# A fused attention and mixture-of-experts block: expert tile pairs cut in two halves and spread over 98 steps, scatters at three a step

## The chip, the core and the metric

The kernel runs on one core of a Trainium2 chip. Its time is the device time of one execution in microseconds (us); the kernel before takes 1445.82 us, the median of three runs (1444.02 to 1447.47).

## What is computed

One transformer block on x of shape (4, 1024, 256), all in float32: a layer norm without weights, then attention and a mixture of experts, both on the normed rows, and the sum of all three.

```python
xn = layernorm(x)
# attention: 16 heads of 16, rotary embedding, softmax over all 1024 keys
qkv = xn @ W_qkv + b_qkv
out = softmax(q @ k.T / sqrt(16)) @ v            # per batch and head
attn = out @ W_out + b_out
# mixture of experts: 16 experts, 4 per token, 256 -> 128 -> 256
scores = sigmoid(xn @ w_gate.T)                   # top 2 of 4 groups, then top 4 experts
g, u = silu(xn @ w1_e.T), xn @ w3_e.T
routed = sum over the 4 experts of weight * ((g * u) @ w2_e.T)
shared = (silu(xn @ w1s.T) * (xn @ w3s.T)) @ w2s.T
return x + attn + routed + shared
```

## The kernel before

**Steps.** Attention is the frame. There are 4 batches of 4 groups of 4 heads, and a group takes 16 steps, so 256 steps in all. `Attention.step` (line 1329) writes one of them. It issues four score products `ps` with the exponential on ScalarE behind each (`exp_one`, line 1170) and four products `pm` of the next group with their row maxima on VectorE behind them (`max_one`, line 1125): half of these eight at the start, half at the end. In the middle, in `between`, it runs the step's *units*: pieces of other work that are handed in as closures. Behind the second half comes `av_part`, the product of the exponentials of the step before with the values. It is written whole if the next step has a unit; otherwise it is cut in two, and the second part goes into the middle of that next step.

**What sets the order.** Every TensorE instruction is kept in the order in which it is written (`Kit.pe`, line 289); TensorE never runs a later unit before an earlier one. The same holds for most of SyncE's transfers (`Kit.sp`, line 295), while the expert loads are placed behind the last transfer written (`issue_after(k.last_sp)`, line 876). All PSUM tiles come from one pool of eight banks.

**Units.** The function `pieces` (line 219) lists the units of a step. First stand attention's own (the projection of the next batch at every second step, its transposes three steps later, the maxima's transposes, the normalisation of a finished group, the output projection); then the shared expert; then the routed experts. The shared expert has 16 blocks of 256 rows with three units each (`shared_block`, line 789): two `hidden` and a `last`. The first 36 units come from step 10 on at three in seven steps (until step 92), the other 12 once the routed experts are done, at two in five steps.

**The routed experts** take four stages.

1. The routing, computed from step 9 on, gives each token's four slots in a buffer `xs` in HBM in which the rows lie sorted by expert.
2. From step 33 on, `put` (line 848) scatters rows into `xs`: 128 indirect DMAs of 128 rows, issued by GpSimd, two a step, so the last one is in step 96. Each is tied to one of the step's maxima or exponentials as its pace (`Kit.paced`).
3. From step 98 on, 72 *pairs* of expert tiles (256 rows each) are worked off, one a step, by `expert_units` (line 871). The unit `pair_of(i)` (line 922) holds, in this order: `outer(i - 1)`, the second product `exy` of the pair before, whose stationary operand is that pair's `gu`; `load(i + 2)`, the rows and the two experts' weights; `turn(i + 1)`, the transposes `ext` of the next pair's rows; `hidden` of pair i (line 759). The last unit is `outer(71)`, at step 170.
4. From step 171 on, `get` (line 940) gathers the results from `ys`, 128 indirect DMAs, two a step (one a step from step 240 on), and `add` sums them on VectorE.

**Inside `hidden`.** Sixteen matmuls `ph_r` are followed by three instructions in a row: tanh on ScalarE (line 776), and two on VectorE (lines 777 and 779). The second of these writes `gu_r`.

```python
th = self.ff.tile([P, SL], F32, name=f"th_{tag}", tag="th")
nc.scalar.activation(th, ph[:, 0, :], AF.Tanh, scale=0.5)
nc.vector.scalar_tensor_tensor(th, th, 1.0, ph[:, 0, :], ALU.add, ALU.mult)
gu = self.ff.tile([P, SL], F32, name=f"gu_{tag}", tag="gu", bufs=3)
nc.vector.tensor_tensor(gu, th, ph[:, 1, :], ALU.mult)
```

Of the kernel before, what the change touches and what calls it, by code (L numbers as in the profile page):

```python
# [20 lines left out]
NT = B * TT  # L21
# [4 lines left out]
TOPK_G, TOPK = 2, 4  # L26
# [6 lines left out]
PAIRS = (NT * P * TOPK // P + E - 1 + R - 1) // R  # L33
# [5 lines left out]
PROJECT = 29  # L39
ROUTE_FROM = 9  # L40
PUT_FROM = 33
TILES_FROM = 98
SHARED = ((10, 36),)
GET_AHEAD = 3
FILL_FROM, FILLS = 9, 8
FFN_AHEAD = 3
# [3 lines left out]
def kernel(  # L50
# [160 lines left out]
    beside = Beside(k, xnT, ff)  # L211
    routing_tensor = []
    routing = route(k, rt_pool, logits, routing_tensor)
    shared = beside.shared_units()
    n_put = NT * TOPK
    done = {"shared": 0}
    tiles, ex = None, None

    def pieces(step):

        nonlocal tiles
        now = norm.pieces(step, att.own(step))
        while routing_tensor:
            now.append(routing_tensor.pop(0))
        due = 0
        if SHARED[0][0] <= step:
            due = min(SHARED[0][1], 1 + (step - SHARED[0][0]) * 3 // 7)
        if tiles is not None and not tiles:
            due = min(len(shared), SHARED[0][1] + (step - TILES_FROM - PAIRS) * 2 // 5)
        while done["shared"] < due:  # L230
            now.append(shared[done["shared"]])
            done["shared"] += 1
        if step == TILES_FROM:
            tiles = beside.expert_units(ex.enter_context(ex_pool()))
        if tiles:
            now.append(tiles.pop(0))
            if not tiles:
                done["tiles"] = step
        return now

    def ex_pool():
        return tc.tile_pool(name="ex", bufs=2, side="right")
# [6 lines left out]

    ex = ExitStack()  # L250
    now = pieces(0)
    for step in range(STEPS):
        beside.tick()
        norm.moves(step)
        if step in k.at_step:
            with tc.issue_after(k.last_exp):
                k.at_step[step]()

        bits = []
        if routing is not None and step >= ROUTE_FROM:  # L260
            bits += [advance] * (1 if step >= PUT_FROM else 2 if k.ranking else 3)
        if step >= PUT_FROM and beside.put_next < n_put:
            assert k.slots_known
            bits[:0] = [beside.put] * 2
        if step > done.get("tiles", STEPS):
            if beside.got == 0:
                ex.close()
                beside.rows = att.rows = ctx.enter_context(
                    tc.tile_pool(name="gp", bufs=4, side="right")
                )  # L270
            for _ in range(2 if step < STEPS - 2 * TT else 1):
                bits += [beside.get, beside.add]
        then = pieces(step + 1) if step + 1 < STEPS else []
        att.step(now, bool(then), bits)
        now = then
# [461 lines left out]
class Beside:  # L737
# [109 lines left out]

    def put(self):
        k, nc, tc = self.k, self.nc, self.tc
        i = self.put_next  # L850
        self.put_next += 1
        t, kk = divmod(i, TOPK)
        q = t // QT
        if i == 0:
            self.fetch(0)
            self.fetch(1)
        elif i % (QT * TOPK) == 0 and q + 1 < NT // QT:
            self.fetch(q + 1)
        put = nc.gpsimd.indirect_dma_start(  # L859
            out=k.xs,  # L860
            out_offset=bass.IndirectOffsetOnAxis(ap=k.slot_i[:, t, kk : kk + 1], axis=0),
            in_=self.rows4[q][:, t % QT, :],
            in_offset=None,
        )
        k.paced(put.ins)

        tc.add_to_no_dep_group("put", put.ins)
        tc.declare_no_dep(put.ins, group="put", reason="rows of their own")


    def expert_units(self, ex):
        k, nc, tc = self.k, self.nc, self.tc
        got, xTs, gus = {}, {}, {}

        def load(i):
            with tc.issue_after(k.last_sp):
                xg = ex.tile([P, R, C], F32, name=f"xg_{i}", tag="xg")
                nc.sync.dma_start(
                    out=xg, in_=k.xs[i * SL : (i + 1) * SL, :].rearrange("(r p) c -> p r c", r=R)
                )  # L880
                w = ex.tile([P, R, WE], F32, name=f"w_{i}", tag="w", bufs=3)
                for r in range(R):
                    n = i * R + r
                    e = nc.sync.value_load(k.tile_e[0:1, n : n + 1], min_val=0, max_val=E - 1)
                    last = nc.sync.dma_start(out=w[:, r, :], in_=k.we[bass.ds(e * P, P), :])
            k.last_sp = last.ins
            got[i] = (xg, w)

        def turn(i):
            xg = got[i][0]  # L890
            pt = k.bank([P, NC_, R, P], f"ext_{i}")
            for c in range(NC_):
                for r in range(R):
                    k.pe(nc.tensor.transpose(pt[:, c, r, :], xg[:, r, c * P : (c + 1) * P], k.ident))  # L894
            xT = self.ff.tile([P, QT, C], F32, name=f"xT_{i}", tag="st")
            xTs[i] = xT[:, :NC_, :]
            nc.scalar.copy(xTs[i], pt.rearrange("p c r n -> p c (r n)"))  # L897

        def outer(i):
            py = k.bank([P, R, C], f"exy_{i}")  # L900
            for r in range(R):
                k.pe(
                    nc.tensor.matmul(  # L903
                        py[:, r, :], lhsT=gus[i][:, r * P : (r + 1) * P],
                        rhs=got[i][1][:, r, 2 * NC_ * F :], start=True, stop=True,
                    )
                )
            y = self.ff.tile([P, R, C], F32, name=f"y_{i}", tag="y", bufs=3)
            nc.scalar.activation(y, py, AF.Copy, scale=0.5)  # L909
            self.later.append(  # L910
                lambda: k.sp(
                    k.ys[i * SL : (i + 1) * SL, :].rearrange("(r p) c -> p r c", r=R), y
                )
            )

        def gate_and_up(i):
            gu = 2 * NC_ * F
            return [
                got[i][1][:, r, :gu].rearrange("p (n c f) -> n p c f", n=2, c=NC_) for r in range(R)
            ]  # L920

        def pair_of(i):
            def run():
                if i == 0:
                    for n in range(FFN_AHEAD - 1):
                        load(n)
                    turn(0)
                if i:
                    outer(i - 1)
                if i + FFN_AHEAD - 1 < PAIRS:  # L930
                    load(i + FFN_AHEAD - 1)
                if i + 1 < PAIRS:
                    turn(i + 1)
                gus[i] = self.hidden(xTs[i], gate_and_up(i), f"r{i}")
            return run

        return [pair_of(i) for i in range(PAIRS)] + [lambda: outer(PAIRS - 1)]


    def get(self):  # L940
# [513 lines left out]
```

## Time and profile before

| | |
|---|---|
| median of three runs | 1445.82 us |
| the profiled execution, its own time | 1442.6 us |
| its span, first to last instruction | 1440.8 us |
| mean granted TensorE clock | 0.995 |
| PE busy | 1407.5 us, 98% of the span |
| PEld (weight loads) busy | 685.6 us, 48% |
| VectorE (DVE) busy | 924.8 us, 64% |
| ScalarE (ACT) busy | 792.8 us, 55% |
| GpSimd (POOL) busy | 423.2 us, 29% |
| HBM traffic | 141 GB/s over the span |

The profile is taken in one execution. "PE" is TensorE's matmuls, "PEld" its weight loads, which overlap them. The row of a group of instructions gives its line in the kernel, the engine, the operation, the tiles written and read, how many there are, the busy time, the mean length of one in ns, and the idle time of the engine just before them with what ended it. In a timeline each row has its start and length in us, the engine and line, and in brackets the engine's idle time before it with its releaser. A float32 matmul shows as two instructions, a transpose as one.

The time of a step is read from the trace as the distance between the first `ps` matmuls of two steps. By this, step 46 begins at 335.5 us, step 81 at 499.3, step 98 at 577.5, step 171 at 1101.8, and step 240 at 1386.6. A step without any unit takes 3.53 us if the next has none either and 3.95 us if the next has one; a step with an expert pair and no other unit takes 6.42 us.

### The profile page before, as it was taken

To read this page: it belongs to the slowest core of one execution; us is meant where nothing else is said; L and a number is where in the kernel's file an instruction comes from. 1 tells how busy PE (TensorE), PEld (TensorE's weight loads), DVE (VectorE), ACT (ScalarE), POOL (GpSimd) and SP (SyncE) were. 2 spreads that over 40 slices of the span, in tenths; PEclk is the share of its full clock that TensorE was granted. 3 is DMA by queue.
4 is the path that set the end of the run, shared out by engine and by line. 5 is a ranking of instruction groups with operands and counts; after the bars stand their busy time and mean duration, and the time that the engine had idled before them with its cause. 6 is when DMAs were issued, how large, how long until landed. Compare 5 with 4: busy or idle time off the path is not lost.

```text
span 1440.8 us, 26647 instructions
## 1 busy us (share of the span) xinstructions
PE 1407.5 (98%) x9870; PEld 685.6 (48%) x9870; DVE 924.8 (64%) x1682; ACT 792.8 (55%) x1638; POOL 423.2 (29%) x498
## 2 busy tenths in 40 slices
PE   7699999999999999999999999999999999999998
PEld 4343344444444343566656665655665434433333
DVE  5667967667766676444555545555445888899941
ACT  5565554555554555555555555555555555566675
POOL 5401511574534546321000000001223444455400
PEclk9899999999999999999999999999999999999999
DMA  5132763333232223445666666665451334333310
GB/s 183 37 111 102 257 250 114 103 125 101 98 133 94 88 87 134 133 150 182 203 214 197 217 194 205 196 207 183 147 174 54 107 118 129 108 110 108 103 44 30
DMA packets 136673, 199.15 MB, mean 138 GB/s; under 512 B 13920, under 2 KB 99040, under 8 KB 136288
## 3 DMA queue, kind: packets, MB, share of 16 engines
q1 hardware_dynamic: 103088, 137.78, 29.8%
q0 software_dynamic: 12288, 33.57, 7.5%
q10 hardware_dynamic: 21168, 26.10, 5.2%
q8 instruction: 78, 1.28, 0.4%
q14 instruction: 51, 0.42, 0.1%
HBM read 124.01 MB, written 79.69 MB: 141 GB/s over the span
## 4 chain that ended last, share of the span: by engine, by line
PE 94%; ACT 3%; DVE 1%; DMA 0%; issue 0%; SPq 0%; ACTq 0%; DVEq 0%
PE pm L1135 22%; PE ps L1177 19%; PE av L1202 18%; PE ph_r L769 9%; PE exy L903 5%; PE ph_s L769 4%; PE pqk L1044 4%; PE ext L894 2%; PE pso L818 2%; PE py L1272 2%; PE pv L1044 2%; PE ptr L1118 2%; PE po L1226 1%; PE pmt L1158 1%; DVE mx L1143 1%; ACT other L373 1%
## 5 line engine op out<-in xcount | busy, mean ns | idle before, releaser
L1186 ACT ACTIVATE es<-ps 128x512 f32<-128x512 f32 x1024 | 555.0, 596 | 413.3 <-PE ps L1177 225.5
L1143 DVE TENSOR_REDUCE mx<-pm 128x1 f32<-128x512 f32 x1024 | 660.5, 684 | 181.2 <-PE pm L1135 115.3
L1135 PE MATMUL pm<-kT,qT 32*128 32x512 f32 x1792 | 522.8, 646 | 8.3 <-ACT kT L1123 5.6
L1177 PE MATMUL ps<-q,kT 32*128 32x512 f32 x1792 | 505.1, 640 | 0.9 <-DVE q L1163 0.8
L1202 PE MATMUL av<-es,vv 128*32 128x512 f32 (+1 forms) x2560 | 287.0, 519 | 0.0
L1177 PEld LDWEIGHTS ps<-q,kT 32*128 32x128 f32 x1792 | 142.3, 183 | 169.2 <-ACT es L1186 86.8
L1135 PEld LDWEIGHTS pm<-kT,qT 32*128 32x128 f32 x1792 | 157.0, 185 | 75.8 <-issue 24.9
L1202 PEld LDWEIGHTS av<-es,vv 128*32 128x32 f32 x2560 | 51.2, 108 | 239.6 <-issue 215.5
L859 POOL DMA_INDIRECT xs<-rows,slot_i x128 | 123.7, 967 | 125.3 <-DVE mx L1143 108.1
L950 POOL DMA_INDIRECT yg<-ys,slot_i x128 | 121.7, 951 | 127.6 <-DVE mx L1143 123.2
L777 DVE SCALAR_TENSOR_TENSOR th_r<-th_r,ph_r 128x256 f32<-128x256 f32 x72 | 30.3, 421 | 195.4 <-ACT th_r L776 195.4
L1082 POOL TENSOR_TENSOR rot<-qk,sin_sb 128x256 f32<-128x256 f32 x56 | 39.5, 726 | 369.4 <-DVE qk L1065 369.2
L769 PE MATMUL ph_r<-xT,w 128*128 128x128 f32 x1152 | 140.5, 275 | 0.5 <-ACT xT L897 0.5
L769 PEld LDWEIGHTS ph_r<-xT,w 128*128 128x128 f32 x1152 | 134.4, 192 | 0.8 <-ACT xT L897 0.7
L1135 PE MATMUL pm<-qkT,qkT 32*128 32x512 f32 x256 | 78.6, 640 | 1.3 <-DVE mx L1143 1.3
L903 PE MATMUL exy<-w,gu_r 128*128 128x256 f32 x288 | 77.3, 391 | 0.0
L1177 PE MATMUL ps<-q,qkT 32*128 32x512 f32 x256 | 75.3, 640 | 0.3 <-DVE gu_s L779 0.3
L776 ACT ACTIVATE th_r<-ph_r 128x256 f32<-128x256 f32 x72 | 27.6, 383 | 81.3 <-PE ph_r L769 81.3
L903 PEld LDWEIGHTS exy<-w,gu_r 128*128 128x128 f32 x288 | 50.0, 190 | 28.7 <-issue 19.7
L967 DVE SCALAR_TENSOR_TENSOR sum<-yg,wk,sum 128x256 f32<-128x256 f32 x128 | 61.4, 479 | 0.0
L909 ACT ACTIVATE y<-exy 128x512 f32<-128x512 f32 x72 | 43.7, 607 | 17.7 <-PE exy L903 17.4
L1036 POOL MEMSET vv<- 128x128 f32 x4 | 1.3, 316 | 143.2 <-ACT es L1186 143.2
(175 smaller groups left out, 1259.3 us busy)
## 6 DMA issues: line engine op xcount, KB each, us to landing
w<-we SPq DMA_DIRECT2D x144, 384.0 KB
xs<-zero ACTq DMA_DIRECT2D x8, 2304.0 KB
xg<-xs SPq DMA_DIRECT2D x72, 256.0 KB
ys<-y SPq DMA_DIRECT2D x72, 256.0 KB
acc<-acc SPq DMA_DIRECT2D x14, 512.0 KB
xb<-in_x_dram SPq DMA_DIRECT2D x16, 256.0 KB
acc<-xb SPq DMA_DIRECT2D x16, 256.0 KB
we<-in_w_dram ACTq DMA_DIRECT2D x4, 1024.0 KB
```

The costliest lines, as they stand in the source:

```text
L769: nc.tensor.matmul(ph[:, n, at], lhsT=w[n][:, c, :], rhs=xT[:, c, at], start=(c == 0), stop=(c == NC_ - 1),)
L859: put = nc.gpsimd.indirect_dma_start(out=k.xs, out_offset=bass.IndirectOffsetOnAxis(ap=k.slot_i[:, t, kk : kk + 1], axis=0), in_=self.rows ...
L903: nc.tensor.matmul(py[:, r, :], lhsT=gus[i][:, r * P : (r + 1) * P], rhs=got[i][1][:, r, 2 * NC_ * F :], start=True, stop=True,)
L909: nc.scalar.activation(y, py, AF.Copy, scale=0.5)
L950: get = nc.gpsimd.indirect_dma_start(out=self.yg[:, kk, :], out_offset=None, in_=k.ys, in_offset=bass.IndirectOffsetOnAxis(ap=k.slot_i[:, ...
L967: nc.vector.scalar_tensor_tensor(sm[:, 0, :], yg[:, kk, :], k.wk[:, t, kk : kk + 1], sm[:, 0, :], ALU.mult, ALU.add)
L1044: nc.tensor.matmul(ps[half][:, :w], lhsT=self.xnT[b][:, c, n0 : n0 + P], rhs=self.wqkv_sb[:, c, half * HALF : half * HALF + w], start=(c = ...
L1135: nc.tensor.matmul(ps, lhsT=self.qT[b, g // 2][rows, g % 2, qt * P : (qt + 1) * P], rhs=self.kT[b, g // 2][rows, g % 2, hf * HALF : (hf + ...
L1143: k.pace = nc.vector.tensor_reduce(out=self.mx_of[b, g, qt // 4][hf][:, qt % 4, j, :], in_=ps, axis=AX.X, op=ALU.max,).ins
L1177: nc.tensor.matmul(ps, lhsT=self.kT[b, g // 2][rows, g % 2, kc * P : (kc + 1) * P], rhs=self.q2[b, g, qh][rows, :], start=True, stop=True,)
L1186: k.last_exp = nc.scalar.activation(e, ps, AF.Exp, scale=DH**-0.5).ins
L1202: nc.tensor.matmul(av[32 * j : 32 * j + 32, cols], lhsT=self.vv[b][:, kc, h * VS : h * VS + 32], rhs=es[j][:, cols], start=(kc == 0), stop ...
```

## The change

The 72 pairs are cut into two units each: `around(i)` has the second product of the pair before, the load and the transposes, and `inner(i)` has `hidden`. With the last `outer` these are 145 units. They start at step 81 in place of 98, and by step `s` as many as `1 + (s - 81) * 144 // 98` have been handed out, so one or two a step, the last of them at step 179. The scatters go at two a step up to step 45 and at three from step 46 on, so that the last three are in step 79. The remaining shared units and the gathers follow the end of the tiles: the gathers start at step 180, and 8 of the 128 come after step 239, at one a step, until step 247. Nothing else changes: the same instructions run, with the same operands.

```diff
-TILES_FROM = 98
-SHARED = ((10, 36),)
+PUT_MORE = 46
+TILES_FROM, TILE_STEPS = 81, 98
+SHARED_FROM, SHARED_FIRST = 10, 36
...
-            due = min(len(shared), SHARED[0][1] + (step - TILES_FROM - PAIRS) * 2 // 5)
+            due = min(len(shared), SHARED_FIRST + (step - TILES_FROM - TILE_STEPS) * 2 // 5)
...
         if step == TILES_FROM:
             tiles = beside.expert_units(ex.enter_context(ex_pool()))
         if tiles:
-            now.append(tiles.pop(0))
+            due = 1 + (step - TILES_FROM) * (2 * PAIRS) // TILE_STEPS
+            while tiles and done["halves"] < due:
+                now.append(tiles.pop(0))
+                done["halves"] += 1
             if not tiles:
                 done["tiles"] = step
...
-            bits[:0] = [beside.put] * 2
+            bits[:0] = [beside.put] * (2 if step < PUT_MORE else 3)
...
     def put(self):
         k, nc, tc = self.k, self.nc, self.tc
+        if self.put_next == NT * TOPK:
+            return
...
-        def pair_of(i):
+
+        def around(i):
             def run():
                 if i == 0:
                     for n in range(FFN_AHEAD - 1):
...
                     load(i + FFN_AHEAD - 1)
                 if i + 1 < PAIRS:
                     turn(i + 1)
+            return run
+
+        def inner(i):
+            def run():
                 gus[i] = self.hidden(xTs[i], gate_and_up(i), f"r{i}")
             return run
 
-        return [pair_of(i) for i in range(PAIRS)] + [lambda: outer(PAIRS - 1)]
+        units = []
+        for i in range(PAIRS):
+            units += [around(i), inner(i)]
+        return units + [lambda: outer(PAIRS - 1)]
```

More of the change, by code (lines that the diff above doesn't have):

```diff
@@ L215 @@
     n_put = NT * TOPK
-    done = {"shared": 0}
+    done = {"shared": 0, "halves": 0}
     tiles, ex = None, None
@@ L225, in pieces @@
         due = 0
-        if SHARED[0][0] <= step:
-            due = min(SHARED[0][1], 1 + (step - SHARED[0][0]) * 3 // 7)
+        if SHARED_FROM <= step:
+            due = min(SHARED_FIRST, 1 + (step - SHARED_FROM) * 3 // 7)
         if tiles is not None and not tiles:
-            due = min(len(shared), SHARED[0][1] + (step - TILES_FROM - PAIRS) * 2 // 5)
+            due = min(len(shared), SHARED_FIRST + (step - TILES_FROM - TILE_STEPS) * 2 // 5)
         while done["shared"] < due:
```

## The prediction

> **What bounds the kernel.** I first read the page's busy rows.
>
> ```profile
> PE 1407.5 (98%) x9870; PEld 685.6 (48%) x9870; DVE 924.8 (64%) x1682; ACT 792.8 (55%) x1638; POOL 423.2 (29%) x498
> ```
>
> TensorE is busy in 98% of the span; no other engine comes above 64%. But a busy PE is a modelled figure, so the second view is the timeline of one step that carries an expert pair, TensorE's rows alone, from the end of the step's first half to its end. Columns: start and length in us, engine, line, operation.
>
> ```profile
> 728.40 1.13 PE L903 MATMUL exy<-w,gu_r 128*128 128x256 f32 x4
> 729.37 0.60 PE L894 MATMUL ext<-ident,xg 128*128 128x128 f32 x4
> 729.80 1.95 PE L769 MATMUL ph_r<-xT,w 128*128 128x128 f32 x16
> 731.68 0.69 PE L1135 MATMUL pm<-kT,qT 32*128 32x512 f32 x1
> ...
> 732.75 1.06 PE L1202 MATMUL av<-es,vv 128*32 128x512 f32 x8
> ```
>
> Each row starts before the one above has drained. Start to start, `exy` costs 0.97 us, `ext` 0.43, `ph_r` 1.88, the second half's eight score matmuls 1.07 and the value product 1.00; with the first half's 1.07 (727.33 to 728.40) that is 6.42 us, the measured step. So TensorE's own work fills a pair step without a hole. The same view of the waits, for TensorE between 600 and 1090 us, lists none. What is added to TensorE's queue there, work or waiting, is added to the time in full; what only changes its place gives nothing.
>
> **The step that the change breaks.** In the same step I read ScalarE's and VectorE's timelines, at the end of `hidden`.
>
> ```profile
> 731.79 0.38 ACT L776 ACTIVATE th_r<-ph_r 128x256 f32<-128x256 f32 x1 [1.15 <-PE ph_r L769]
> ```
> ```profile
> 732.21 0.42 DVE L777 SCALAR_TENSOR_TENSOR th_r<-th_r,ph_r 128x256 f32<-128x256 f32 x1 [2.39 <-ACT th_r L776]
> 732.66 0.42 DVE L779 TENSOR_TENSOR gu_r<-th_r,ph_r 128x256 f32<-128x256 f32 x1
> ```
>
> `gu_r` is ready at 733.08, 1.33 us behind the last `ph_r` (731.75). All three had waited for TensorE, not for a queue of their own, so 1.33 is a pure latency. In all 72 pairs it is 1.33. Today nobody waits for it: `exy` of this pair comes in the next step's middle, 1.74 us later at 734.82, and the score and value products stand between.
>
> After the change a step can hold `inner(i)` and then `around(i + 1)`, whose first work is `outer(i)`: `exy` reads the `gu_r` whose `ph_r` has only just been issued. Units are numbered evenly for `around`, oddly for `inner`, and step 81 + k ends with unit 144k // 98. Listing k = 0 to 98 gives 145 units in 99 steps: 46 steps with two, of which 22 begin with an even number (the old order, harmless) and **24 begin with an odd one**: 84, 88, 92, 96, 99, 103, 107, 111, 118, 122, 126, 130, 133, 137, 141, 145, 148, 152, 156, 160, 167, 171, 175 and 179 (`inner(71)`, then the last `outer`). There TensorE stands still with `ext`, the second half's scores and the value product queued behind `exy`; ScalarE and VectorE wait for those.
>
> **Price of one such wait.** Within a run of equal matmuls the next starts 0.11 us behind the last one (1.88 us by 16, with the change to the scores in it). The last `ph_r` starts at 731.48, so `exy` could start at 731.59. With the wait it starts at 733.08 plus a hand-over; between the links of this chain that is 0.03 to 0.04 us (731.75 to 731.79). So 1.53 us. `exy`'s stationary operand is `gu_r` itself, so its weight load (190 ns by its row) can't be loaded ahead either; up to 0.19 more. Lower end: the next instruction's present start, 731.68, to 733.08, 1.40 us. I take 1.55, between 1.40 and 1.72. 24 x 1.55 = **+37.2 us** (33.6 to 41.3). Nothing gives it back: the step's other TensorE work is behind it in order, and later steps have no TensorE waits to shorten.
>
> **Steps that are filled.** An empty step has four late score matmuls (the eight of its first half take 1.31 us instead of 1.07) and a cut value product (2 x 0.57 instead of 1.00). A step with a unit pays about 0.2 us for changing between score and full matmuls: eight shared matmuls take 1.92, eight times 0.216 is 1.73. From the step lengths, a frame without units is 3.95 us (next step has units) or 3.53 (it has none); with units, that change included and the units' pure work not, 3.34 or 2.91. For steps 12 to 239 I count the kinds before and after: filled before filled 129 to 141, filled before empty 35 to 32, empty before filled 35 to 32, empty before empty 29 to 23. 12 x 3.34 - 3 x 2.91 - 3 x 3.95 - 6 x 3.53 = **-1.7 us**. It pays for cutting a pair in two as well, since each half's change is in the 3.34.
>
> **Three scatters a step.** GpSimd does one in 1.27 us when it is behind (starts 433.24, 434.50, 435.77), so three take 3.8 us; steps 46 to 79 last (494.6 - 335.5) / 34 = 4.7 us on average, but empty ones 3.5 to 4.0. 102 scatters take 130 us of 159, and the shared blocks' additions (1.3 us each, plus the wait for their input, 5.1 us before the one at 430.5) some 20 more. GpSimd is nearly full but keeps up, within one or two steps. It is tied to no TensorE work until step 81, where `turn(0)` needs the scattered rows. Before, the last scatter starts at 572.05, the load of the first rows is issued at 574.47, and `ext` starts at 579.89 without a wait: 7.8 us from scatter to use. After, on schedule, the last scatter starts 3.4 us into step 79, and `ext` stands 1.07 us into step 81: 3.95 + 4.64 + 1.07 - 3.4 = 6.3 us. A lag of GpSimd comes on top. Bounds: 0 (the load took less than its cover) and 8 (one lag of 6.5 us and the missing 1.5); I take **+2 us**, once, nearer to the low end because the last addition before falls in step 73. The wait of 0.47 us of the first `ph_r` for `xT` goes, since they fall in two steps: **-0.5**.
>
> **Edits at nothing.** The weight loads keep their distance (issued in `around(i)`, read two pairs later, over 13 us, on a SyncE queue with room); data per us falls with the tiles' rate. Gathers and additions move nine steps later; the last additions come in step 250 beside ScalarE-bound steps of 2.1 to 2.7 us on an idle VectorE, and the stored sums have until the product in step 255, 10 us later. If that cover failed, one store and one load would add some 4 us. The shared block's buffers in steps 81 to 92 leave two of three for `y` and one for `gu`; each is free a step earlier than needed.
>
> **Sum.** 37.2 - 1.7 + 2 - 0.5 = +37.0 us. The profiled execution: span 1440.8 to 1477.8, its time 1442.6 to 1479.6. The median lies 3.2 us above the profiled execution, so 1445.8 becomes **1483 us**.
>
> **Two rules against the rows.** First, the Trainium skill ("TensorE: Matmul & The Clock Gate", section "A second HAM failure mode: psum-queue depth-cycling") says that frequent micro-idles between groups of matmuls can make the clock gate swing to half rate. By it each wait would be followed by at least a 3.4 us window at half clock (the same page's figure), 1.7 us lost, 24 x 1.7 = 41 us more: 1524 us. The trace has one wait of this size in the run:
>
> ```profile
> 441.36 1.12 PE L1135 MATMUL pm<-qkT,qkT 32*128 32x512 f32 x2 [1.28 <-DVE mx L1143]
> ```
>
> In the windows 440 to 442 and 442 to 446 the granted clock is 1.00. I go by the row: single waits of 1.5 us, 15 us or more apart. Second, "Perfetto Trace Analysis", section "Identifying the Most-Contended Engine", wants TensorE judged by the busy share of its weight loads, not of its matmuls. That share is 48%, which reads as room to catch up; the forecast would then be about -2, 1444. The step's sum (6.42 of 6.42 us) says there is no room, and it decides.
>
> **Rivals.**
>
> 1. *It gets faster: the spreading pays and the wait costs nothing.* Place: the 24 steps; the wait would have to be swallowed by time that TensorE loses today on late banks. For it: TensorE loses 0.25 us in empty steps, 1.28 at 440 us and 0.33 at 481. Price: -1.7 - 0.5, and up to -1.6 if both of these go: 1442 to 1444. It decides if TensorE's idle in a step with `inner` ahead of `around` is below 0.1 us. Against it: the pair steps have no such loss. Chance 0.07.
> 2. *Half a wait.* The first eight `ph_r` are all that tanh needs, and they end 0.89 us earlier. If tanh began there, the wait would be near 0.65: 24 x 0.65 = 15.6, so 1461. Against it: tanh starts 0.04 us behind the last of the sixteen in every pair. Chance 0.05.
> 3. *GpSimd falls behind.* Three scatters against short steps pile up a lag of several steps, and the tiles' start waits for it beyond 8 us, or late shared additions hold VectorE and so the banks. It comes on top: 1490 to 1500. Against it: the 150 of 159 us above. Chance 0.08.
> 4. *The clock swings*, as priced: 1524. Chance 0.02.
>
> The forecast has 0.78: 33.6 - 2.2 = +31.4 to 41.3 - 2.2 + 8 = +47.1, 1477 to 1493. The range goes on to rival 2 and into rival 3: 1464 to 1494. Within 0.2% of before (about what this measurement can tell from no change, 3 us) and faster share rival 1: 0.04 and 0.03. Slower: 0.93.
>
> **What would show it.** In the changed trace TensorE's waits list `exy` behind VectorE's `gu_r`, 24 times, 1.4 to 1.7 us each, in the steps named; their sum is the loss. Steps with `around` alone take about 4.5 us, with `inner` alone 5.0, with `around` then `inner` 6.4, with `inner` then `around` near 8. The clock stays at 1.00. A wait of `ext` near step 81 shows the scatters. I am wrong if `exy` starts right behind `ph_r` in these steps, or if the steps after them are shorter than 4.5 us.

## The result

The changed kernel takes 1508.71 us (median of six runs, 1507.79 to 1511.66) where the kernel before takes 1444.99 on the same chip: 1.0443 times as long, with a 95% interval of 1.0433 to 1.0453. The forecast was 1483, with 1464 to 1494 as its range. The profiled execution took 1508.26; its span is 1506.5 us against 1440.8.

The page of the changed kernel opens with the busy rows that the prediction also read first.

```profile
PE 1436.7 (95%) x9798; PEld 690.0 (46%) x9798; DVE 929.5 (62%) x1682; ACT 794.0 (53%) x1638; POOL 423.2 (28%) x498
```

TensorE's share has fallen from 98% to 95%, so about 70 us of the span are now without matmuls, against some 33 before. The view of TensorE's waits names half of that (engine, line, what was waited for: total, times, longest, in us).

```profile
PE exy L909 <- DVE gu_r L783: 34.2, 24, 1.5
```

This is the forecast wait, 24 times. One of them in full, in step 118, from the timeline (start, length, engine, line; in brackets the idle time before and what ended it):

```profile
788.98 0.38 ACT L780 ACTIVATE th_r<-ph_r 128x256 f32<-128x256 f32 x1 [0.92 <-PE ph_r L773]
789.39 0.42 DVE L781 SCALAR_TENSOR_TENSOR th_r<-th_r,ph_r 128x256 f32<-128x256 f32 x1 [1.09 <-ACT th_r L780]
789.85 0.42 DVE L783 TENSOR_TENSOR gu_r<-th_r,ph_r 128x256 f32<-128x256 f32 x1
790.32 0.73 PEld L909 LDWEIGHTS exy<-w,gu_r 128*128 128x128 f32 x4 [1.57 <-DVE gu_r L783]
790.32 1.13 PE L909 MATMUL exy<-w,gu_r 128*128 128x256 f32 x4 [1.38 <-DVE gu_r L783]
```

The chain that the prediction drew from the kernel before stands here link by link, and TensorE is idle for its length.

**Where the time went.** I laid the two traces side by side by the starts of their steps. The difference grows by 1.4 us up to step 46, the first that the change touches, by **27.2 in steps 46 to 80** and by 39.6 in the 24 steps named in the prediction (with no other unit in them they take 8.07 us where a pair's step takes 6.42; 24 times 1.65). All others are the remainder, -2.5: 65.7 us. So the forecast has its large term right, and misses a second one of 27 us, which was to be 2. That one falls in few steps: 51, 62, 63, 68 and 75 lose 3.3 to 6.5 us each, four others (53, 55, 57 and 76) 1.1 to 1.9.

**What those steps look like.** The timeline of the changed kernel in step 51, some rows of four engines.

```profile
355.95 0.69 DVE L1157 TENSOR_REDUCE mx<-pm 128x1 f32<-128x512 f32 x1 [0.64 <-PE pm L1149]
356.92 0.96 POOL L865 DMA_INDIRECT xs<-rows,slot_i  x1 [0.50 <-DVE mx L1157]
357.37 0.69 DVE L1157 TENSOR_REDUCE mx<-pm 128x1 f32<-128x512 f32 x1 [0.72 <-PE pmt L1172]
...
358.28 0.59 PE L1191 MATMUL ps<-q,kT 32*128 32x512 f32 x1
358.34 0.96 POOL L865 DMA_INDIRECT xs<-rows,slot_i  x1 [0.46 <-DVE mx L1157]
358.79 0.69 DVE L1177 TENSOR_TENSOR q<-qT,pmt 128x512 f32<-128x512 f32 x1 [0.73 <-PE pso L822]
...
358.80 1.07 PE L1216 MATMUL av<-es,vv 128*32 128x512 f32 x8
...
359.79 0.69 PE L1191 MATMUL ps<-q,kT 32*128 32x512 f32 x1
...
360.29 0.69 DVE L829 SCALAR_TENSOR_TENSOR xb<-pso,xb 128x512 f32<-128x512 f32 x1 [0.81 <-PE av L1216]
360.32 1.58 ACT L1200 ACTIVATE es<-ps 128x512 f32<-128x512 f32 x3 [3.32 <-PE av L1216]
```

VectorE takes up its inputs from TensorE one by one, 1.42 us apart (355.95, 357.37, 358.79), and ScalarE's exponential starts at 360.32 although the last `ps` had ended at 358.87 by its row. A matmul's end is modelled, but TensorE keeps its order, and behind that `ps` it had already begun `av` (358.80) and the next step's `ps` (359.79). In the trace's semaphore events (the signals by which one engine tells another that it is done) TensorE's come singly ahead of two of these starts (357.35 and 358.77), and from 360.21 on five within 0.17 us, while VectorE's own come within 0.02 us of the ends of its rows. So what is late is the news that a matmul is done. TensorE stands still a little later, because its banks come free late; the waits view spreads that over many small rows.

Each of these steps comes at the end of a **long row of scatters** on GpSimd. In the changed kernel six rows have starts 1.26 to 1.30 us apart without a break: six scatters from 366.0, from 375.5 and from 385.2, ten from 409.2, eight from 445.9, nine from 485.2. The row ahead of step 51's loss has small breaks: eight scatters from 348.7 to 358.3, 1.26 to 1.67 us apart. The loss is larger behind the longer ones: 1.1 to 1.4 us behind each six, 4.5 behind the eight, 7.8 behind the ten and 8.4 behind the nine. The clock falls too (views by windows; columns: stretch, its length, busy time and instructions of PE, PEld, DVE, ACT and POOL, granted clock, DMA share, GB/s).

```profile
400.00:416.00 16.00, 16.00 (x119) 6.55 (x119) 10.41 (x19) 8.88 (x17) 8.56 (x10) 1.00 0.34 113
416.00:436.00 20.00, 18.98 (x80) 8.54 (x80) 7.54 (x14) 4.94 (x10) 9.10 (x10) 0.74 0.35 121
436.00:452.00 16.00, 16.00 (x116) 6.97 (x119) 11.35 (x20) 8.36 (x16) 10.37 (x12) 1.00 0.58 198
```

The records of the clock show four stretches at half rate in steps 46 to 80, of 3.4, 10.2, 3.4 and 10.2 us, each begun behind such a stall. At half rate 27.3 us do the work of 13.7, so the clock accounts for up to 13.6 of the 27.

The kernel before has the same thing small. The row that the prediction quoted for the clock, TensorE's wait of 1.28 us at 441.36, stands right behind the longest row of scatters in that trace:

```profile
431.94 0.99 POOL L859 DMA_INDIRECT xs<-rows,slot_i  x1 [0.15 <-DVE mx L1143]
...
433.24 0.96 POOL L859 DMA_INDIRECT xs<-rows,slot_i  x1 [0.30 <-issue]
...
437.04 0.96 POOL L859 DMA_INDIRECT xs<-rows,slot_i  x1 [0.30 <-DVE mx L1143]
...
438.30 0.96 POOL L859 DMA_INDIRECT xs<-rows,slot_i  x1 [0.30 <-issue]
```

Six scatters in a row, and the one other loss of that region (0.33 us at 481) follows a row of five. The prediction used the row to judge the clock and did not ask what had caused the wait.

### The profile page after: what moved, and what is told of

Same layout as the page of the kernel before. It is cut to its first block, busy times and chain, and to the rows that moved or that the text cites. A ratio compares the mean times of both kernels' runs of the same rounds, so it can differ in the third digit from the quotient of the medians.

```text
span 1506.5 us, 26429 instructions
## 1 busy us (share of the span) xinstructions
PE 1436.7 (95%) x9798; PEld 690.0 (46%) x9798; DVE 929.5 (62%) x1682; ACT 794.0 (53%) x1638; POOL 423.2 (28%) x498
## 3 DMA queue, kind: packets, MB, share of 16 engines
q8 instruction: 78, 1.28, 0.4%
## 4 chain that ended last, share of the span: by engine, by line
PE 88%; ACT 4%; DVE 3%; issue 2%; POOL 2%; DMA 1%; POOLq 0%; SPq 0%; DVEq 0%; ACTq 0%
PE pm L1149 19%; PE ps L1191 18%; PE av L1216 16%; PE ph_r L773 9%; PE exy L909 5%; PE ph_s L773 4%; PE pqk L1058 3%; PE ext L900 2%; PE pso L822 2%; PE py L1286 2%; POOL yg L964 2%; PE ptr L1132 2%; PE pv L1058 2%; PE pmt L1172 1%; PE po L1240 1%
## 5 line engine op out<-in xcount | busy, mean ns | idle before, releaser
L1191 PE MATMUL ps<-q,kT 32*128 32x512 f32 x1792 | 516.9, 644 | 2.3 <-DVE q L1177 0.8
L1149 PEld LDWEIGHTS pm<-kT,qT 32*128 32x128 f32 x1792 | 153.5, 185 | 73.0 <-issue 30.3
L1149 PE MATMUL pm<-qkT,qkT 32*128 32x512 f32 x256 | 91.4, 685 | 0.7 <-DVE mx L1157 0.6
L1191 PE MATMUL ps<-q,qkT 32*128 32x512 f32 x256 | 80.3, 663 | 1.4 <-DVE q L1177 1.0
L909 PEld LDWEIGHTS exy<-w,gu_r 128*128 128x128 f32 x288 | 49.7, 189 | 59.4 <-issue 23.2
L803 POOL TENSOR_TENSOR xb<-xb,bo_sb 128x512 f32<-128x512 f32 x16 | 20.6, 1293 | 146.3 <-DMA xb<-in_x_dram 127.5
```

The costliest lines, as they stand in the source:

```text
L909: nc.tensor.matmul(py[:, r, :], lhsT=gus[i][:, r * P : (r + 1) * P], rhs=got[i][1][:, r, 2 * NC_ * F :], start=True, stop=True,)
L1149: nc.tensor.matmul(ps, lhsT=self.qT[b, g // 2][rows, g % 2, qt * P : (qt + 1) * P], rhs=self.kT[b, g // 2][rows, g % 2, hf * HALF : (hf + ...
L1191: nc.tensor.matmul(ps, lhsT=self.kT[b, g // 2][rows, g % 2, kc * P : (kc + 1) * P], rhs=self.q2[b, g, qh][rows, :], start=True, stop=True,)
```

## The experiments

Each run stands beside runs of the kernel before on the same chip. Losses of single steps are differences of step lengths against the profiled kernel before. Experiments 1 to 8 and the halves in 9 are one execution each. Executions of the kernel before lie up to 5 us apart (1442.46 to 1447.47 outside experiment 10), so anything smaller is read from step lengths alone.

**1. The scatters alone.** The kernel before, three scatters a step from step 46, tiles as before.

```diff
-            bits[:0] = [beside.put] * 2
+            bits[:0] = [beside.put] * (2 if step < 46 else 3)
```

> The kernel before with one edit: three scatters a step from step 46 on; the tiles stay whole pairs from step 98 on. In the changed kernel steps 46 to 80 lost 27.2 us. Theory S (the scatters are what TensorE loses time to in those steps): 1445 + 27, so 1466 to 1478 us, with the loss in steps 46 to 80 and none of TensorE's waits at exy. Rival T (the loss before step 81 comes with the tiles' early start, whose six weight loads go out at 481 us, or with another order of the units): 1442 to 1449.

Measured: 1467.94 us beside 1445.56, +22.4. Steps 46 to 80 lose 23.2, all later steps nothing, and no `exy` waits. The second loss is the scatters' alone; tiles and order have no part in it.

**2. The order alone undone.** The changed kernel, but a step stops handing out halves behind an `inner`, so that `around` never follows in the same step.

```diff
                 done["halves"] += 1
+                if done["halves"] % 2 == 0:
+                    break
```

> The changed kernel with one edit: a step stops taking halves behind an inner, so no step has inner(i) and then around(i + 1). Theory W (24 waits of exy for gu_r, 1.65 us each by the step lengths, 8.07 against 6.42): 1508.7 - 39.6, so 1466 to 1472 us, and no wait of exy for gu_r. Rival (what stands behind exy waits for something else as well, so the time only moves): above 1490.

Measured: 1468.09, 40.6 less than the changed kernel. The row of `exy` behind `gu_r` is gone from TensorE's waits; 28.2 us up to step 81 stay. The 24 waits are therefore worth their 40 us, and the pairs' spreading without them gives 4.9 us back after step 81.

**3. Rate or row.** The kernel before with its two scatters a step handed out as eight every fourth step, or four every second one: the same mean rate, other rows.

```diff
-            bits[:0] = [beside.put] * 2
+            bits[:0] = [beside.put] * (8 if (step - PUT_FROM) % 4 == 0 else 0)
```

> The kernel before with one edit: eight scatters in every fourth step in place of two in every step, the same 128 over the same 64 steps. In the changed kernel each of the eight runs of six or more scatters back to back (1.265 us apart) is followed by long steps, 27.2 us in all, 3.4 a run. Theory S-run (a long run back to back holds TensorE up): 16 runs, 3 to 4 us each, so 1445 + 48 to 64: 1493 to 1509 us. Rival S-rate (three a step over the whole stretch are too many for GpSimd or the queue, runs don't matter): the rate is that of before, 1442 to 1450.

> The kernel before with one edit: four scatters in every second step in place of two in every step. The kernel before has two runs of four (at 361.4 and 560.0 us) without a long step behind them, and a run of six and one of five that are followed by one. Theory S-run with its threshold at five or six: 1442 to 1452 us. If shorter runs hold TensorE up too: 32 runs, 1 us or more each, so above 1475. Rival S-rate: 1442 to 1450.

Measured: eight in a row 1498.82 (+53.3), four in a row 1455.74 (+10.2). Since the rate is that of the kernel before, it is the row that costs. The rows of eight that stayed whole lost 2.6 to 6.6 us each. Four came out above what was expected of it: the rows of exactly four lose nothing, with one exception of 1.4 us; most of the rest comes where GpSimd had fallen behind an addition and two fours ran together, seven from 434.0 and eight from 477.4, with 3.8 and 3.7 us lost behind them.

**4. GpSimd busy without DMAs.** The kernel before, in steps 110 to 157 every fourth step 32 small memsets.

```diff
+        if 110 <= step < 158 and step % 4 == 2:
+            bits += [beside.idle_work] * 8
...
+        for _ in range(4):
+            fill = self.nc.gpsimd.memset(self.scratch, 0.0)
```

> The kernel before with GpSimd kept busy in steps 110 to 157: every fourth step 32 small memsets in a row, about as long as eight scatters, and no DMA more. The memsets write a tile that nobody reads, work that the reference does not have. Theory D (it is the issue of DMAs in a row that holds TensorE's signals up): no loss in these steps, 1443 to 1448. Theory B (it is GpSimd busy without a gap, through a port or a bus that it shares): 12 bunches lose about what a bunch of eight scatters lost, 3 to 4 us each, 1480 to 1495.

Measured: 1443.72 beside 1445.42. No step of these loses anything. But each bunch holds GpSimd for 6.6 us in two halves of 3.28, with 1.1 to 4.6 us between them, which is less than an unbroken row of eight scatters (10 us). So this run alone doesn't clear a GpSimd that is busy without a break; experiment 7 does.

**5. The other direction.** The gathers of the kernel before in bunches of eight every fourth step.

```diff
-                bits += [beside.get, beside.add]
+            if (step - 171) % 4 == 0:
+                bits += [beside.get] * 8
+            bits += [beside.add] * 2
```

> The kernel before with its gathers in bunches of eight every fourth step from step 171 on, the additions at two a step as before. Gathers go the other way, from DRAM into SBUF. Theory G (any run of indirect DMAs that GpSimd issues without a gap delays TensorE's signals): some 13 bunches lose 3 to 4 us each, 1480 to 1500. Theory W (only the writes to DRAM do it): no loss beyond 2 us, 1444 to 1448.

Measured: 1544.01, +98.6. That is more than expected: 16 bunches at some 6 us, with 99 us of the trace at half clock (up to 49 of the loss). The sums that use the gathered rows are not the cause: VectorE has no wait for a gathered row from step 171 on. The sign is that of step 51: in the bunch from 1338.8 on TensorE's signals come singly at 1344.45, 1345.88, 1347.31 and 1348.71, and then several from 1350.19. Reading from HBM costs as well as writing to it.

**6. Rows or volume.** Twelve bunches of eight more scatters, in steps 110 to 154 of the kernel before, with full rows of 1 KB or with a quarter of each.

```diff
+        if 110 <= step < 158 and step % 4 == 2:
+            bits += [beside.idle_put] * 8
...
+            out=k.xd,
+            out_offset=bass.IndirectOffsetOnAxis(ap=k.slot_i[:, t, kk : kk + 1], axis=0),
+            in_=k.w1s_sb[:, 0, 0:256],
```

For the quarter rows the last line reads `0:64`.

> The kernel before with twelve bunches of eight scatters more, one bunch every fourth step from 110 to 154, each scatter 128 rows of 1 KB into a DRAM tensor that nobody reads (work that the reference does not have). Theory L (a run of six or more delays TensorE's signals, whatever it writes and whatever step it stands in): each bunch loses 3 to 5 us, 1480 to 1505. Rival (it takes the short steps without a pair, or a bank that a late addition holds): in these steps, with a pair in most, under 1 us a bunch, 1445 to 1457.

> The same twelve bunches as in the kernel with full rows, but each scatter writes 128 rows of 256 bytes, a quarter of the data with the same number of rows. Theory R (the number of rows, and the instruction's own work, sets the price): about the loss of the full rows. Theory V (the volume of data does): under a third of that loss; if the full rows lose 48 us, under 16.

Measured: 1513.64 and 1513.22 beside 1444.49, +69.2 and +68.7. A quarter of the data costs the same. One bunch of the quarter rows in its timeline:

```profile
714.21 0.96 POOL L857 DMA_INDIRECT xd<-w1s_sb,slot_i  x1 [0.30 <-issue]
715.47 0.96 POOL L857 DMA_INDIRECT xd<-w1s_sb,slot_i  x1 [0.30 <-issue]
716.39 0.60 ACT L1206 ACTIVATE es<-ps 128x512 f32<-128x512 f32 x1 [2.87 <-issue]
716.74 0.96 POOL L857 DMA_INDIRECT xd<-w1s_sb,slot_i  x1 [0.30 <-issue]
...
718.00 0.96 POOL L857 DMA_INDIRECT xd<-w1s_sb,slot_i  x1 [0.30 <-issue]
720.65 1.09 ACT L1206 ACTIVATE es<-ps 128x512 f32<-128x512 f32 x2 [3.67 <-remote]
720.70 1.29 DVE L1163 TENSOR_REDUCE mx<-pm 128x1 f32<-128x512 f32 x2 [5.82 <-remote]
721.30 2.78 PEld L773 LDWEIGHTS ph_r<-xT,w 128*128 128x128 f32 x16 [3.84 <-ACT es L1206]
```

The last four of the eight scatters are on GpSimd's rows. ScalarE and VectorE stand idle for 3.67 and 5.82 us, and TensorE's weight loads for 3.84, until 2.7 us behind the start of the last one. The DMA engines are all but idle meanwhile; the same run by windows:

```profile
706.00:716.00 10.00, 10.00 (x79) 5.72 (x76) 5.53 (x10) 4.23 (x8) 5.33 (x6) 1.00 0.67 220
716.00:722.00 6.00, 1.87 (x13) 1.23 (x12) 1.30 (x3) 1.95 (x4) 2.35 (x3) 1.00 0.08 20
722.00:726.00 4.00, 4.00 (x25) 2.64 (x26) 1.41 (x4) 1.09 (x3) 0.00 (x0) 0.57 0.90 321
```

In the stall the DMA share is 0.08 at 20 GB/s, and the queues that fetch instructions carry nothing from 712 to 722, so a late fetch is not the cause. The half clock comes in the window behind it, when TensorE has work again.

**7. A pause in the row.** The twelve bunches with full rows, each parted into four and four by six small memsets.

```diff
-            bits += [beside.idle_put] * 8
+            bits += [beside.idle_put] * 4 + [beside.pause] + [beside.idle_put] * 4
```

> The kernel with twelve bunches of eight scatters of full rows (1513.6), each bunch now parted into four and four by six small memsets, some 1.3 us of GpSimd, so that the same rows are written in the same steps (again work that the reference does not have). Theory L (what counts is the length of an unbroken run, with four still free): the loss of 69 us goes nearly all, 1443 to 1460. Rival A (what counts is the number of rows in some ten us, a backlog that drains slowly; a pause as long as one scatter takes one scatter's worth off): half to nine tenths of the loss stay, 1480 to 1508.

Measured: 1456.98 beside 1442.98, +14.0 where the unbroken bunches had +69. The same rows in the same steps, so their number in ten us is not what costs. GpSimd's rows of the first bunch:

```profile
680.71 0.96 POOL L863 DMA_INDIRECT xd<-w1s_sb,slot_i  x1 [0.30 <-issue]
681.98 0.96 POOL L863 DMA_INDIRECT xd<-w1s_sb,slot_i  x1 [0.30 <-issue]
682.94 1.22 POOL L855 MEMSET scratch<- 128x64 f32 x6
684.72 0.97 POOL L863 DMA_INDIRECT xd<-w1s_sb,slot_i  x1 [0.56 <-issue]
```

Fourth to fifth start are 2.74 us apart instead of 1.27. A bunch then costs at most 2.0 us, and no half clock follows. In the first bunch GpSimd, memsets included, is never idle for more than 0.56 us in the 10.4 us from the first scatter's start to the eighth's, and 0.5 us is lost. So a GpSimd that is busy without a break is not the cause; the DMAs that it issues in a row are. In the quarter rows the bunches differ by themselves in the same way: nine unbroken ones lose 6.4 us each, one with 1.89 us between the fourth start and the fifth 4.5, two with 4.17 us 1.6.

**8. Both repairs.** The changed kernel with the order repaired, and two memsets behind every third scatter.

```diff
+        if i % 3 == 1 and i > 26:
+            for _ in range(2):
+                pause = nc.gpsimd.memset(self.scratch, 0.0)
+                k.paced(pause.ins)
```

> The changed kernel with both repairs: a step's loop over units ends after an inner, and GpSimd gets two small memsets behind every third scatter, so that its scatters start in groups of three with a gap, at the same three a step. Theory L (a long unbroken run of scatters, six or more, delays TensorE's completion signals): the groups never reach six, so the 28 us that the order repair left before step 81 go: 1440 to 1447, about the kernel before or a little under it. Theory Q (it is the rate of three scatters a step, or GpSimd's load, that costs; a gap changes nothing or makes GpSimd later still): 1465 to 1480.

Measured: 1455.62 beside 1445.42, outside what either theory expected. Most of the 28 us up to step 81 go, but not all: a stall in step 55 and a half clock of 6.8 us behind it cost 5.7. It comes in a stretch (365.39 to 388.85) where no more than three scatters stand in a row and each third start is 1.89 us ahead of the next, so such short breaks do not always help. The pauses also make GpSimd late for the tiles' start. TensorE's waits say so:

```profile
PE ext L907 <- DMA xg<-xs: 4.8, 1, 4.8
```

The last scatter starts at 510.74, `ext` at 516.01, and another half clock follows. That is the wait that the prediction had looked for near step 81. In the changed kernel itself the last scatter starts at 523.63 and `ext` at 528.92 without a wait: the same 5.3 us, here just covered.

**9. Other ways to a gain.** First, the shared expert's units cut into halves like the pairs, to fill more of the empty steps of the kernel before; then the changed kernel with the order repair, two and three scatters a step in turn, and tiles from step 89 over 90 steps.

```diff
-SHARED = ((10, 36),)
+SHARED = ((10, 72),)
```

> The kernel before with the units of the shared expert cut into halves, as the change did with the pairs: 72 by step 94, six every seven steps, then 24, four every five steps, so that fewer steps are empty. The theory of the prediction (an empty step loses about 0.4 us to late score matmuls, cutting costs about 0.2): a gain of 0 to 9 us, 1436 to 1446. Rival: each cut holds a bank longer and costs the change between kinds of matmul twice, so nothing or a loss, 1446 to 1455. No wait of exy for gu_r is expected, and the scatters stay at two a step.

```diff
-TILES_FROM, TILE_STEPS = 81, 98
+TILES_FROM, TILE_STEPS = 89, 90
...
-            bits[:0] = [beside.put] * (2 if step < PUT_MORE else 3)
+            bits[:0] = [beside.put] * (2 if step < PUT_MORE else 2 + step % 2)
```

> The changed kernel with the order repair, scatters at two and three a step in turn instead of three from step 46 on (the last one in step 86), and tiles from step 89 on, spread over 90 steps, so that they end in the same step. GpSimd now has about 3.2 of 4.7 us a step to fill. Theory L (only unbroken runs of six and more cost): few such runs are left, behind the additions that wait for their input, 2 to 8 us in all, and with the 5 us that spreading the pairs earned in the order repair: 1440 to 1448. Rival: the losses go with the number of scatters before the tiles' start, however paced: 1455 to 1468.

Measured: the halves give 1445.40 beside 1445.42. They lose 6.8 us in steps 10 to 32 and win 5.2 later; whether the early loss (with a half clock of 6.8 us at 152.0) belongs to them one run can't tell. The later start takes 1453.12, 1.0070 (1.0043 to 1.0098), a miss. Its rows of scatters are at most five long, but its runs lie between 1447.8 and 1458.1; the profiled one is the quickest of them, with losses of 0.4 to 1.7 us behind rows of five and 1.9 behind four and three with 1.7 us between their starts. Thinner scatters alone leave rows at the edge of what is free.

**10. The change repaired.** The order repair, three scatters a step already from step 40, and the two memsets behind every fourth scatter.

```diff
-PUT_MORE = 46
+PUT_MORE = 40
...
+        if i % 4 == 3 and i > 13:
+            for _ in range(2):
+                pause = nc.gpsimd.memset(self.scratch, 0.0)
+                k.paced(pause.ins)
```

> The changed kernel with the order repair, three scatters a step from step 40 on instead of 46 (so the last one is due in step 77 instead of 79), and two small memsets behind every fourth scatter. Theory L with a lag at the tiles' start (in the kernel with both repairs the scatters came late, ext of the first pair waited 4.8 us and the steps 80 and 81 lost about 10 us): the six earlier scatters take some 8 us off that wait, no run is longer than four, the spreading keeps its 5 us: 1438 to 1448. Rival (the steps 80 and 81 lose for another reason, or the pauses let GpSimd fall behind as much as the earlier start wins): 1450 to 1462.

> The kernel before, with nothing but two small memsets on GpSimd behind every fourth scatter; scatters stay at two a step, pairs whole and from step 98 on. Theory L: the two losses that the kernel before has itself (step 69 is 2.4 us longer and step 77 1.65 us longer than in the repaired change, each behind a run of five or six scatters) go, 3 to 4 us: ratio 0.997 to 0.998, and the spreading of the pairs adds little to the repaired change's 4.5. Rival: the gain of the repaired change is the spreading's, and pauses alone give nothing: ratio 0.999 to 1.001.

> The repaired change again (order repair, scatters at three a step from step 40, pauses behind every fourth), on the same chip as the kernel with pauses alone, so that the two can be set side by side. Both theories: ratio 0.996 to 0.998. If the spreading earns its own 5 us, it stays 3 us or more below the kernel with pauses alone; if not, the two agree within 1.5 us.

Measured: the repaired change takes 1434.60 beside 1439.10, **0.9970 (0.9959 to 0.9980)**, and in the second set 1435.11 beside 1438.39, 0.9977 (0.9966 to 0.9987). The kernel before with the pauses alone takes 1439.18, 1.0004 (0.9995 to 1.0013). Busy rows of the repaired change:

```profile
PE 1400.6 (98%) x9790; PEld 679.6 (47%) x9790; DVE 927.2 (65%) x1682; ACT 792.3 (55%) x1638; POOL 432.3 (30%) x556
```

Its scatters stand in rows of four from step 46 on, up to five rows one behind the other. No step from 46 to 80 loses more than 0.5 us, the granted clock is 1.00 there, and the first `ext` doesn't wait. Against the kernel with pauses alone, the two profiles part after step 81: 11.7 us gained up to step 181 against a loss of 0.5, then 5.9 to 6.3 lost where the other gains 0.9, net 4.9 to 5.3. The timed runs say 4.1 (1439.18 less 1435.11). So the gain is the spreading's. In the profile the pauses alone also clear the two late steps of the kernel before (69 and 77, 4.0 us); the timed runs show no gain from that, which stays unexplained.

## Why the prediction was wrong

- **The bound** held: what was put into TensorE's queue came out in full in the time.
- **The 24 steps** held in number, place and mechanism: they are the steps listed, and 24 waits of 1.4 to 1.5 us. By step length each costs 1.65, where the sum had 1.55 (1.40 to 1.72); 39.6 us in place of 37.2.
- **Filled empty steps and the wait for `xT`**, -1.7 and -0.5: what the steps without scatters or `exy` waits give back is -2.5.
- **Step lengths** foretold as 4.5, 5.0, 6.4 and near 8 us are 4.63, 5.12, 6.42 and 8.07.
- **Three scatters a step: this term failed.** It was set at +2 us (0 to 8) on the ground that GpSimd keeps up and "is tied to no TensorE work until step 81". It does keep up within one step (the last scatter starts 0.8 us into step 80), and no `ext` is late: 5.3 us from that scatter to `ext` were enough, where the sum allowed for a need of up to 7.8. But it is tied to TensorE without any dependency in the code: behind a long row of indirect DMAs, six or more in this kernel, TensorE's completions reach ScalarE and VectorE late. In place of 2 stand 27.2 us in the change, 23.2 of them in the scatters alone (experiment 1); the row, not the rate, makes them (3, 7), whatever the direction (5) and the volume (6).
- **Rival 3**, GpSimd falling behind, named the right instructions and the wrong reason; with 1490 to 1500 it was also too low. Its late `ext` appeared only once pauses had slowed GpSimd down (8).
- **The clock**, foretold at 1.00 and measured 0.985 over the span. Weighing the rule of the Trainium skill ("TensorE: Matmul & The Clock Gate", section "A second HAM failure mode: psum-queue depth-cycling") against one wait of 1.28 us was right for what it was asked: none of the 24 waits is followed by half clock. The stalls behind scatters are several waits on end, and behind them the half clock came, in stretches of 3.41, 6.83 and 10.24 us. So the rule has its place in this kernel, but not where the prediction had put its price, an estimate from that page's window of 3.4 us.
- **Edits at nothing**: two small losses come with the later gathers, which had been costed at 0. Step 244 loses 1.2 us, where a sum waits 1.31 us for a gathered row and attention's own work on VectorE stands behind it. Step 206 loses 1.8 us at the end of a row of four gathers (1319.15 to 1322.92), with TensorE's signals late as in step 51.

The sum with the measured terms: 39.6 + 27.2 - 2.5 = 64.3, and 1.4 of the start, 65.7.

## What to carry to other kernels

When GpSimd issues indirect DMAs beside a TensorE-bound loop, count how many stand in an unbroken row, not only whether GpSimd keeps up: here scatters by fours were nearly free and unbroken eights cost 2.6 to 8 us each, and a pause of some 1.5 us in the middle of twelve eights took their loss from 69 us to 14. Where halves of a unit are spread over steps, look for the step in which a producer comes right before its consumer; ending the step behind the producer cost nothing and was worth 40 us. And ask of every wait in the profile before, however small, what ended it and what stood in front of it: the 1.28 us at 441 was the missed term in small.

## What the runs showed of the hardware

- A row of indirect DMAs issued by GpSimd without a break (starts 1.27 us apart, 128 rows each) delays TensorE's completions for ScalarE and VectorE: 1.42 us apart in the changed kernel, up to 5.8 us of idle time in one go. Unbroken rows of eight lose 2.6 to 6.6 us in experiment 3 and 6.4 on average beside the pairs; rows of four lose little or nothing (at most 1.8 us, the gathers at step 206).
- The price goes with the data rows of a scatter (128 in every one here), or with the instruction itself, not with the bytes (+69.2 and +68.7 us for 1 KB and 256 bytes a row), and not with GpSimd's being busy (0.5 us lost in a bunch in which memsets between the fours left it idle for 0.56 us at most). The Trainium skill ("DMA: Bandwidth & Descriptors", section "SWDGE vs HWDGE vs iDMA") says that GpSimd writes a pair of descriptors for each operation into rings in SBUF. A price by rows would fit that; no run here shows the path on which TensorE's signals are held up, so the mechanism stays open.
- How long a pause must be stays open too. In steps 46 to 80 of the repaired change rows of four with 1.89 us from the fourth start to the next lost nothing, five rows on end; beside the pairs one bunch with that same distance, but no memset in it, still lost 4.5 us, and in experiment 8 rows of three with that distance and with memsets ended in a stall. What makes the difference was not tried.
- Each stall that cost over 3 us in the changed kernel, and each of the ten costliest bunches of full rows, was followed by half clock for 3.41, 6.83 or 10.24 us, some 58 us in the kernel with full rows (up to 29 of its 69). Single waits of 1.5 us, 18 us and more apart, were not.
